# A four-layer graph network in one launch: stages cut into small steps, one fixed turn for all five engines, and a sigmoid formed from exp

## The chip, the cores and the metric

The kernel runs on one core of a Trainium2 chip. A core has a matrix engine (TensorE, in the profile PE, with its weight loads as PEld), a vector engine (VectorE, DVE), an engine for activation functions (ScalarE, ACT), a general engine (GpSimd, POOL) and one that starts transfers (SyncE, SP). Each works through its own row of instructions in order and waits on semaphores for the others. The metric is the device time of one launch in microseconds. Before the change it was 2602.46 us, the median of three runs (2601.76 to 2607.09).

## The reference

The input x is 128 graphs of 128 nodes with 256 features, in single precision. One 128x128 adjacency `adj` serves all. Each of the four layers adds its result to x; each starts with a normalization over the features and a relu:

```python
h = jnp.maximum(_layernorm(x, axis=-1), 0.0)
# layer 0: messages along adj and its transpose, three sigmoid gates per node
msg_in   = (origin*adj @ h + edge_bias)         * sigmoid(h @ gate_weight + bias_gate)
msg_out  = (origin.T*adj @ h + out_edge_bias)   * sigmoid(h @ out_gate_weight + out_bias_gate)
msg_loop = h * sigmoid(h @ loop_gate)
x = x + relu(msg_in + msg_out + msg_loop)
# layer 1: causal attention over the nodes with adj as additive mask, then Wo
# layer 2: three products, each followed by adj*S (S = 1), relu after the first two
#          widths 256 -> 512 -> 1024 -> 256
# layer 3: adj normalized by degree, then Linear(256 -> 512), batch norm over all
#          graphs and nodes, relu, Linear(512 -> 256), batch norm, no relu
```

(The code is shortened; names are those of the reference.) Both batch norms need sums over all graphs, so there is a first pass up to the input of the first batch norm, then a second pass over all graphs, and a last one that writes the output.

## The kernel before

Four graphs make a group; there are 32 groups, and the first pass works on several at once: while layer 2 of group g runs, layer 1 of group g+1, layer 0 of group g+2 and layer 3 of group g-1 fill in between. Each layer is a Python generator, and a `yield` ends a stage. A string gives the order in which stages are emitted (capitals for stages of the current streams, `b` and `d` for those that start the next ones):

```python
TURN = "CCBBCBACDBCABBCABDBACBDDACDCADDCDCBDCADBCBACABCbCBbCBBCBBCBBCBCbBCd"
FIRST = "CCCB" + TURN[2:].replace("C", "", 1)
...
for g in range(NG):
    if g + AHEAD < NG:
        load_x(g + AHEAD)
    ...
    stream = {
        "A": part(layer0, g + 2), "B": bs, "C": layer2(g), "D": ds,
        "b": part(layer1, g + 2), "d": layer3(g),
    }
    for k in FIRST if g == 0 else TURN if g < LAST else FINAL:
        next(stream[k], None)
```

The emitted order is only a wish: a scheduler that comes after it may move an instruction ahead of others of its engine. A few instructions are kept in emitted order by `keep_in_program_order` (the relus of `norm`, the transposes of `cut`), the stores of z are put behind certain loads by `follow`, and `in_turn`, which chains every new instruction to the one before it on its engine, is used for TensorE in the opening stage alone.

All wide products use Strassen's scheme in Winograd's form: seven products in place of eight, in three accumulators (px, py, pz; 2 KB per partition each, one of eight PSUM banks):

```python
def seven(product, put, shape, name, pool=None):
    def kept(pb, i):                       # copy an accumulator away, ScalarE
        t = (pool or w).tile(shape, FP, tag="kept", name=f"{name}_t{i}", bufs=6)
        nc.scalar.copy(t, pb)
        return t
    px = bank(shape, f"{name}_x");  product(0, px, True);  t1 = kept(px, 1);       yield
    py = bank(shape, f"{name}_y");  product(1, py, True);  put((0, 0), py, t1);    yield
    pz = bank(shape, f"{name}_z");  product(4, pz, True);  t5 = kept(pz, 5);       yield
    product(5, px, False);  t2 = kept(px, 2);                                      yield
    product(2, pz, False);  put((0, 1), pz, t2);                                   yield
    product(6, px, False);  put((1, 1), px, t5);                                   yield
    product(3, px, False);  put((1, 0), px, None);                                 yield
```

(Here put several to a line.) A product that goes on in px or pz must wait until the copy or addition of the one before has read it. `put` adds on VectorE and, in layer 2, applies relu on ScalarE. `sums` makes the four sums of quarter matrices that the scheme needs, on VectorE.

`norm` makes the statistics on VectorE, the inverse square root in four small steps on GpSimd, and h by four relus on ScalarE. Three matrices must be turned (h before layer 1, the gated adjacency m of layer 0, the softmax p of layer 1); `swap` sends them out to memory and back with their 32x32 blocks exchanged, and `cut` turns the blocks on VectorE:

```python
# layer 0, groups 2 and on
nc.vector.scalar_tensor_tensor(gs, h[:, b, :], 1.0, gw[:, i, :], ALU.mult, ALU.mult,
                               accum_out=gl[:, k, i : i + 1])       # 12 per group
nc.vector.tensor_tensor(gl, gl, gate_bias, ALU.add)
gt = small.tile([P, n, 3], FP, tag="gt", name=f"gt_{tail}")
nc.scalar.activation(gt, gl, AF.Sigmoid)
yield
... # m = gt0*ain + gt1*aout + gt2*ident (ScalarE, then VectorE); bias = gt0*eb + gt1*oeb
swap(flatT, f"cc_{g}")
yield; ...; yield
cut(cmb.rearrange("p b n -> p (b n)"), flatT, G)
yield
for q in range(bs[0] // 2, (bs[-1] + 1) // 2):
    pm = bank([P, 2, D], f"pm_{g}_{q}")
    for r in range(2):
        b = 2 * q + r
        nc.tensor.matmul(pm[:, r, :], cmbT[:, b, :], h[:, b, :], start=True, stop=True)
    half = slice(2 * q, 2 * q + 2)
    nc.vector.tensor_tensor(bias[:, half, :], pm, bias[:, half, :], ALU.add)
```

The softmax of layer 1 uses `AF.Exp` on ScalarE, four times a group. Names in the profile: p_x, p_y, p_z are accumulators of layer 2 (reading uT, us for the second product, h2T, h2s for the third), pu those of its first, pqv of layer 1's query and value product, pz of layer 3; ps and py are attention's scores and output, pm is layer 0's message (line 616) or the mixing by adj before layer 2 (line 449), pmu the mixing after its first product, pg that of layer 3, pr the last step of layer 2.

Of the kernel before, what the change touches and what calls it, by code (L numbers as in the profile page):

```python
# [22 lines left out]
def kernel(  # L23
# [61 lines left out]
    behind = {}  # L85

# [104 lines left out]
    nc.scalar.activation(table, nhalf[:, 0:1], AF.Sigmoid)  # L191
# [168 lines left out]
    def norm(g, layer, bs=ALL):  # L360
# [4 lines left out]
        for k, b in enumerate(bs):  # L365
            nc.vector.bn_stats(st[:, k, :], xt[:, b, :])  # L366
        for k in range(n):
            nc.vector.bn_aggr(mv[:, k, :], st[:, k, :])  # L368
# [10 lines left out]
        def relus(blocks=False, pinned=False):  # L379

            h = tile_of(g, bs, [P, G, D], "h", f"h{layer}_{g}", 3)
            for k, b in enumerate(bs):
# [6 lines left out]
                relu = nc.scalar.activation(  # L389
                    dst, src, AF.Relu, bias=sh[:, k : k + 1], scale=rs[:, k : k + 1]  # L390
                )
                if pinned:
                    tc.keep_in_program_order(relu)
# [19 lines left out]
    fetched = []  # L413

    def follow(i, name):

        tc.add_manual_dep(
            i, name,
            mybir.DependencyInfo(mybir.DependencyClass.NoSync, mybir.DependencyReason.DATA),
            reason="follow",  # L420
        )

    def swap(blocks, name):

        e = blocks.shape[1] // NQ
        home = scratch.tile([NQ, Q, NQ, e], FP, name=name)
        for i in range(NQ):
            nc.sync.dma_start(
                home[:, :, i, :].rearrange("j r e -> r j e"),
                blocks[i * Q : (i + 1) * Q].rearrange("p (j e) -> p j e", j=NQ),  # L430
            )
        nc.sync.dma_start(blocks, home.rearrange("j r i e -> (j r) (i e)"))
        fetched.append(nc.cur_bb.bb.instructions[-1].name)

    def cut(dst, blocks, nb):

        tc.keep_in_program_order(
            nc.vector.transpose(
                dst.rearrange("p (b i c) -> p b i c", b=nb, i=NQ),
                blocks.rearrange("p (i b c) -> p b i c", i=NQ, b=nb),  # L440
            )
        )

    def mixed(dst, src, aT, name, evicts, bs=ALL):

        for c in range(src.shape[-1] // P):
            pm = bank([P, len(bs), P], f"{name}_{c}")
            for k, b in enumerate(bs):
                nc.tensor.matmul(  # L449
                    pm[:, k, :], src[:, b, c * P : (c + 1) * P], aT, start=True, stop=True  # L450
                )
            evicts[c % len(evicts)](columns(dst, c, bs), pm.rearrange("p b n -> p (b n)"))  # L452

    def sums(engine, a, extra, s3=None):
# [5 lines left out]
        engine.tensor_tensor(s1, a21, a22, ALU.add)  # L460
        engine.tensor_tensor(s2, s1, a11, ALU.subtract)
        engine.tensor_tensor(s4, a12, s2, ALU.subtract)
        engine.tensor_tensor(s3, a11, a21, ALU.subtract)
# [38 lines left out]
    def seven(product, put, shape, name, pool=None):  # L502
# [10 lines left out]
        product(0, px, True)  # L513
        t1 = kept(px, 1)
# [3 lines left out]
        put((0, 0), py, t1)  # L518
        yield
        pz = bank(shape, f"{name}_z")  # L520
        product(4, pz, True)
        t5 = kept(pz, 5)
        yield
        product(5, px, False)
        t2 = kept(px, 2)
        yield
        product(2, pz, False)
        put((0, 1), pz, t2)
        yield
        product(6, px, False)  # L530
        put((1, 1), px, t5)
        yield
        product(3, px, False)
        put((1, 0), px, None)
        yield

    def layer0(g, bs=ALL):

        xt, n, tail = X[g], len(bs), f"{g}_{bs[0]}"
        relus = norm(g, 0, bs)  # L540
        if g >= 2:
            yield
        h = relus(pinned=g >= 1)
# [16 lines left out]
        else:  # L560
            gs = w.tile([P, D], FP, tag="gs", name=f"gs_{tail}", bufs=1)
            for k, b in enumerate(bs):
# [5 lines left out]
                if k == n // 2 - 1:  # L568
                    yield
            nc.vector.tensor_tensor(gl, gl, gate_bias, ALU.add)  # L570
        gt = small.tile([P, n, 3], FP, tag="gt", name=f"gt_{tail}")
        nc.scalar.activation(gt, gl, AF.Sigmoid)
# [9 lines left out]
        for k, b in enumerate(bs):  # L582
            nc.scalar.activation(cmb[:, b, :], ain, AF.Copy, scale=gt[:, k, 0:1])
            nc.vector.scalar_tensor_tensor(
# [6 lines left out]
            nc.vector.scalar_tensor_tensor(dst, one, gt[:, k, 2:3], now, ALU.mult, ALU.add)  # L591
        if g >= 2:
            swap(flatT, f"cc_{g}")
        for k, b in enumerate(bs):
            nc.scalar.activation(bias[:, b, :], eb, AF.Copy, scale=gt[:, k, 0:1])
        yield
        for k, b in enumerate(bs):
            nc.vector.scalar_tensor_tensor(
                bias[:, b, :], oeb, gt[:, k, 1:2], bias[:, b, :], ALU.mult, ALU.add
            )  # L600
        mine = slice(bs[0], bs[-1] + 1)
# [10 lines left out]
        for q in range(bs[0] // 2, (bs[-1] + 1) // 2):  # L612
            pm = bank([P, 2, D], f"pm_{g}_{q}")
            for r in range(2):
                b = 2 * q + r
                nc.tensor.matmul(pm[:, r, :], cmbT[:, b, :], h[:, b, :], start=True, stop=True)  # L616
            half = slice(2 * q, 2 * q + 2)
            nc.vector.tensor_tensor(bias[:, half, :], pm, bias[:, half, :], ALU.add)
        yield
# [5 lines left out]
    def layer1(g, bs=ALL):  # L625
# [5 lines left out]
        relus = norm(g, 1, bs)  # L631
        if n == G:
            yield
        h = relus(swapped, n == G)
# [9 lines left out]
        if n == G:  # L644
            yield
            ex = w.tile([P, 4, 1, T // 2], FP, tag="ex", name=f"hs_{g}", bufs=2)
            hs = sums(nc.vector, quarters_t(hT), ex, ex[:, 3])
# [16 lines left out]
        def put(ij, pb, other):  # L664
# [3 lines left out]
            else:  # L668
                nc.vector.tensor_tensor(dst, pb, other, ALU.add)

# [29 lines left out]
        for k, b in enumerate(bs):  # L700
            for c in range(DC):
# [4 lines left out]
                )  # L706
        p = tile_of(g, bs, [P, G, P], "p", f"p_{g}", 1)[:, bs[0] : bs[-1] + 1, :]
        nc.vector.scalar_tensor_tensor(
            p, ps, 1.0 / D**0.5, maskb[:, None, :].to_broadcast([P, n, P]), ALU.mult, ALU.add
        )  # L710
        nmax = small.tile([P, n], FP, tag="nmax", name=f"nmax_{tail}")
        nc.vector.tensor_reduce(nmax, p, AX.X, ALU.max, negate=True)
        psumr = small.tile([P, n], FP, tag="psumr", name=f"psumr_{tail}")
# [10 lines left out]
        if n == G:  # L724
            swap(flat_p, f"pc_{g}")
        rsum = small.tile([P, n], FP, tag="rsum", name=f"rsum_{tail}")
# [11 lines left out]
        for q in halves:  # L738
            py = bank([P, 2, D], f"py_{g}_{q}")
            for r in range(2):  # L740
                b = 2 * q + r
                nc.tensor.matmul(py[:, r, :], pT[:, b - bs[0], :], v_of(b), start=True, stop=True)
            for r in range(2):
# [4 lines left out]
                )  # L748
        yield
        relus = norm(g, 2, bs)  # L750
        if n == G:
            yield
        h = relus(pinned=n == G)
        yield
        mT = tile_of(g, bs, [P, DC, T], "dT", f"mT_{g}", 2)
        mixed(mT, h, a2T, f"pm2_{tail}", (nc.vector.tensor_copy, nc.scalar.copy), bs)
        if n == G:
            ex = w.tile([P, 3, 1, T // 2], FP, tag="ex", name=f"ms_{g}", bufs=2)
            ms = sums(nc.vector, quarters_t(mT), ex)
# [3 lines left out]
        def put(ij, pb, other):  # L763
# [4 lines left out]
            else:  # L768
                nc.vector.tensor_tensor(dst, pb, other, ALU.add)  # L769
                nc.scalar.activation(dst, dst, AF.Relu)  # L770
# [17 lines left out]
        mixed(uT, u, a2T, f"pmu_{tail}", (nc.vector.tensor_copy,), bs)  # L788
        if bs[-1] == G - 1:
            ex = w.tile([P, 3, HC1 // 2, T // 2], FP, tag="us", name=f"us_{g}", bufs=1)  # L790
            US[g] = sums(nc.vector, quarters_t(uT), ex)
        yield

    def layer2(g):
# [8 lines left out]
        def wide(q):  # L803
            def put(ij, pb, other):
# [3 lines left out]
                if other is None:  # L808
                    nc.scalar.activation(dst, pb, AF.Relu)
                    mine = slice(2 * q, 2 * q + 2)  # L810
                    sums(
# [3 lines left out]
                else:  # L815
                    nc.vector.tensor_tensor(dst, pb, other, ALU.add)  # L816
                    nc.scalar.activation(dst, dst, AF.Relu)  # L817
# [7 lines left out]
        def put_s(ij, pb, other):  # L825
# [6 lines left out]
            else:  # L832
                nc.vector.tensor_tensor(dst, pb, other, ALU.add)

        yield from wide(0)
        late = wide(1)
        for _ in range(6 if g == LAST else 7):
            yield next(late)
        third = seven(rows_by_half(h2s, SETS["3"], P), put_s, [P, 2, P], f"p3_{g}")
        yield next(third)  # L840
        yield from late if g == LAST else ()
        yield from third
        for q in range(G // 2):
            pr = bank([P, 2, D], f"pr_{g}_{q}")
            nc.tensor.matmul(pr, a2T, S[0][:, 2 * q : 2 * q + 2, :], start=True, stop=True)  # L845
            nc.vector.tensor_tensor(
                xt[:, 2 * q : 2 * q + 2, :], pr, xt[:, 2 * q : 2 * q + 2, :], ALU.add
            )
        nc.gpsimd.dma_start(X3[g].rearrange("(b n) d -> n b d", n=P), xt)
        yield  # L850

    def layer3(g):
# [3 lines left out]
        for bs in parts:  # L856
            relus = norm(g, 3, bs)
            if g < LAST:
                yield
            h = relus(pinned=g < LAST)  # L860
            yield
        gT = tile_of(g, parts[0], [P, DC, T], "dT", f"gT_{g}", 2)
        for i, bs in enumerate(parts):
            mixed(gT, h, ahT, f"pg_{g}_{i}", (nc.vector.tensor_copy,), bs)
            if g < LAST:
                ex = w.tile([P, 3, 1, T // 2], FP, tag="ex", name=f"gs_{g}", bufs=2)
                gs = sums(nc.vector, quarters_t(gT), ex)
# [4 lines left out]
        def put(ij, pb, other):  # L872
# [13 lines left out]
            if done.count(j) == 2:  # L886
                if g < LAST - 1:
                    for jj in range(2):
                        nc.vector.bn_stats(stats1[:, 2 * j + jj, g, :], z[j][:, jj, :])

        if g < LAST:
            yield from seven(columns_by_half(gs, SETS["b"], 0), put, [P, 2, T // 2], f"pz_{g}")
            at = len(nc.cur_bb.bb.instructions)
            for j in (1, 0):
                nc.sync.dma_start(Z[g][:, 2 * j : 2 * j + 2, :], z[j])
            for i in nc.cur_bb.bb.instructions[at:]:
                for name in fetched[-2:]:
                    follow(i, name)
            yield
            return  # L900
        for i, j in (0, 0), (1, 0), (0, 1), (1, 1):
# [9 lines left out]
            put((i, j), pb, None)  # L911
# [12 lines left out]
    TURN = "CCBBCBACDBCABBCABDBACBDDACDCADDCDCBDCADBCBACABCbCBbCBBCBBCBBCBCbBCd"  # L924
    FIRST = "CCCB" + TURN[2:].replace("C", "", 1)


    FINAL = "CCCCCCCCDCCCCCCCCCCDCCCCDDdDDddDdDdDDdddd"
    US = {}
    AHEAD = 3  # L930

# [12 lines left out]
    for k in FILL:  # L944
# [3 lines left out]
        else:  # L948
            next(stream[k])
# [3 lines left out]
    for _ in range(2):  # L953
        next(bs)
    for g in range(NG):
# [8 lines left out]
        for k in FIRST if g == 0 else TURN if g < LAST else FINAL:  # L964
# [246 lines left out]
```

## Time and profile before

| | |
|---|---|
| median of 3 runs | 2602.46 us |
| span of the profiled execution | 2598.9 us, 40812 instructions |
| first pass, groups 1 to 30 | from about 140 to about 2273 us |
| second and last pass | from about 2330 us to the end |
| HBM traffic | 105 MB read, 99 MB written, 78 GB/s on average |
| loads of ScalarE's function tables | 61 in the loop, 78.3 us of ScalarE |

The profile comes from one execution. Its page gives the busy time of each engine, the span in 40 slices, the chain of work that ended last followed backward, and groups of instructions by line of the kernel. A line such as `L816 DVE TENSOR_TENSOR h2T<-p_z,p_t 128x512 f32<-128x512 f32 x64 | 43.6, 682 | 122.5 <-ACT h L389 108.3` reads: source line 816, on VectorE, writes h2T from p_z and p_t, 64 times; busy 43.6 us in all, 682 ns each; VectorE was idle 122.5 us just before these, 108.3 of it until ScalarE ended h at line 389. A timeline lists instructions by time: start, duration of the run of equal ones, and in brackets the idle time before it with its releaser. In a list of waits stand the total in us, the number of times and the longest. A single-precision matmul of the program stands as two records in the trace.

### The profile page before, as it was taken

To read this page: it belongs to the slowest core of one execution; us is meant where nothing else is said; L and a number is where in the kernel's file an instruction comes from. 1 tells how busy PE (TensorE), PEld (TensorE's weight loads), DVE (VectorE), ACT (ScalarE), POOL (GpSimd) and SP (SyncE) were. 2 spreads that over 40 slices of the span, in tenths; PEclk is the share of its full clock that TensorE was granted. 3 is DMA by queue.
4 is the path that set the end of the run, shared out by engine and by line. 5 is a ranking of instruction groups with operands and counts; after the bars stand their busy time and mean duration, and the time that the engine had idled before them with its cause. 6 is when DMAs were issued, how large, how long until landed. Compare 5 with 4: busy or idle time off the path is not lost.

```text
span 2598.9 us, 40812 instructions
## 1 busy us (share of the span) xinstructions
PE 2520.7 (97%) x14832; PEld 2236.0 (86%) x14832; DVE 1921.9 (74%) x4795; ACT 1259.5 (48%) x2547; POOL 271.5 (10%) x563
## 2 busy tenths in 40 slices
PE   7999999999999999999999999999999999999996
PEld 6788888888888888888888888888888888888875
DVE  7677777777777777777777777877777777558886
ACT  4444444444445444444444454444444444337766
POOL 2110011111001110111111011100111110000001
PEclk9999999999999999999999999999999999999998
DMA  3112211222222112112222222122112221125559
GB/s 133 45 52 66 65 46 54 65 66 58 62 61 66 57 58 66 54 50 61 66 63 60 58 66 58 56 65 59 51 54 66 66 57 49 33 99 217 178 186 388
DMA packets 115180, 206.54 MB, mean 79 GB/s; under 512 B 11538, under 2 KB 77092, under 8 KB 111012
## 3 DMA queue, kind: packets, MB, share of 16 engines
q1 hardware_dynamic: 108404, 180.80, 22.3%
q0 software_dynamic: 6432, 23.07, 2.5%
q8 instruction: 117, 1.92, 0.3%
q14 instruction: 83, 0.68, 0.1%
q10 hardware_dynamic: 144, 0.07, 0.0%
HBM read 105.20 MB, written 98.70 MB: 78 GB/s over the span
## 4 chain that ended last, share of the span: by engine, by line
PE 91%; DVE 4%; ACT 2%; DMA 1%; issue 1%; POOL 0%; SPq 0%; ACTq 0%; DVEq 0%; POOLq 0%
PE p_x L494 16%; PE p_x L477 9%; PE p_z L494 8%; PE pz_x L494 4%; PE p_z L477 4%; PE pmu L449 4%; PE p_y L494 4%; PE po_x L1084 4%; PE pu_x L477 4%; PE pz_z L494 2%; PE pm L616 2%; PE pm L449 2%; PE pqv_x L654 2%; PE pg L449 2%; PE p_y L477 2%; PE pr L845 2%
## 5 line engine op out<-in xcount | busy, mean ns | idle before, releaser
L389 ACT ACTIVATE h<-x,sh,rs 128x256 f32<-128x256 f32 x512 | 265.6, 589 | 69.9 <-POOL sh L375 57.8
L494 PE MATMUL p_x<-uT,w 128*128 128x256 f32 x1024 | 247.0, 379 | 0.0
L509 ACT COPY p_t<-p_x 128x512 f32<-128x512 f32 (+1 forms) x192 | 97.4, 507 | 299.4 <-PE p_x L494 291.2
L494 PEld LDWEIGHTS p_x<-uT,w 128*128 128x128 f32 x1024 | 192.0, 190 | 38.0 <-issue 14.8
L817 ACT ACTIVATE h2T<-h2T 128x512 f32<-128x512 f32 x192 | 120.9, 630 | 198.1 <-DVE h2T L816 198.1
L366 DVE BATCH_NORM_STATS2 st<-x 128x6 f32<-128x256 f32 x512 | 182.2, 411 | 0.2
L564 DVE SCALAR_TENSOR_TENSOR gs<-h,gw 128x256 f32<-128x256 f32 x360 | 151.1, 420 | 41.0 <-ACT h L389 35.6
L372 POOL TENSOR_SCALAR rs<-mv 128x4 f32<-128x4 f32 x124 | 29.7, 240 | 1287.6 <-DVE mv L368 1237.0
L816 DVE TENSOR_TENSOR h2T<-p_z,p_t 128x512 f32<-128x512 f32 x64 | 43.6, 682 | 122.5 <-ACT h L389 108.3
L373 POOL TENSOR_TENSOR rs<-rs,nhalf 128x4 f32<-128x4 f32 x124 | 128.7, 1038 | 0.0
L477 PEld LDWEIGHTS p_x<-w,h2T 128*128 128x128 f32 x1024 | 124.5, 192 | 3.3
L494 PE MATMUL p_z<-us,w 128*128 128x256 f32 x512 | 125.8, 379 | 0.0
L477 PE MATMUL p_x<-w,h2T 128*128 128x128 f32 x1024 | 124.8, 275 | 0.0
L494 PE MATMUL p_x<-us,w_s 128*128 128x256 f32 x512 | 121.3, 379 | 3.0 <-ACT p_t L509 3.0
L494 PE MATMUL p_x<-uT,w_s 128*128 128x256 f32 x512 | 121.5, 380 | 2.0 <-DVE h2T L816 2.0
L494 PE MATMUL p_z<-us,w_s 128*128 128x256 f32 x512 | 121.0, 379 | 0.0
L494 PE MATMUL p_y<-uT,w 128*128 128x256 f32 x512 | 120.9, 379 | 0.0
L449 PE MATMUL pmu<-a2T,u 128*128 128x128 f32 x1024 | 119.6, 275 | 0.0
L452 DVE COPY uT<-pmu 128x512 f32<-128x512 f32 (+1 forms) x132 | 88.4, 674 | 40.7 <-PE pmu L449 40.7
L449 PEld LDWEIGHTS pmu<-a2T,u 128*128 128x128 f32 x1024 | 116.9, 192 | 0.0
L770 ACT ACTIVATE u<-u 128x512 f32<-128x512 f32 x93 | 58.6, 630 | 116.7 <-DVE u L769 116.7
L494 PEld LDWEIGHTS p_y<-uT,w 128*128 128x128 f32 x512 | 97.3, 190 | 13.2
(331 smaller groups left out, 6061.1 us busy)
## 6 DMA issues: line engine op xcount, KB each, us to landing
z<-zo SPq DMA_DIRECT2D x62, 512.0 KB, 4.1
zi<-z SPq DMA_DIRECT2D x31, 1024.0 KB, 4.9
x<-x POOLq DMA_DIRECT2D x32, 512.0 KB, 3.5
x<-in_x_dram SPq DMA_DIRECT2D x31, 512.0 KB, 3.9
hc<-h SPq DMA_DIRECT2D x120, 128.0 KB, 2.5
h<-hc SPq DMA_DIRECT2D x30, 512.0 KB, 3.5
out_dram<-x3i SPq DMA_DIRECT2D x30, 512.0 KB, 10.5
x3i<-x SPq DMA_DIRECT2D x20, 512.0 KB, 6.5
```

The source lines that it names most:

```text
L366: nc.vector.bn_stats(st[:, k, :], xt[:, b, :])
L373: nc.gpsimd.tensor_tensor(rs, rs, nhalf[:, :n], ALU.pow)
L389: relu = nc.scalar.activation(dst, src, AF.Relu, bias=sh[:, k : k + 1], scale=rs[:, k : k + 1])
L449: nc.tensor.matmul(pm[:, k, :], src[:, b, c * P : (c + 1) * P], aT, start=True, stop=True)
L452: evicts[c % len(evicts)](columns(dst, c, bs), pm.rearrange("p b n -> p (b n)"))
L477: nc.tensor.matmul(pb[:, rr, :], a_r[r][:, c, rr * P : (rr + 1) * P], b_r[r][:, c, :wide], start=(first and rr == 0 and c == 0), stop=(c = ...
L494: nc.tensor.matmul(pb[:, jj, :], b_r[r][:, c, at : at + P], a_r[r][:, c, :], start=(first and jj == 0 and c == 0), stop=(c == nk - 1), ski ...
L509: nc.scalar.copy(t, pb)
L564: nc.vector.scalar_tensor_tensor(gs, h[:, b, :], 1.0, gw[:, i, :], ALU.mult, ALU.mult, accum_out=gl[:, k, i : i + 1],)
L770: nc.scalar.activation(dst, dst, AF.Relu)
L817: nc.scalar.activation(dst, dst, AF.Relu)
L1084: nc.tensor.matmul(pb, BW2R[r][:, c, :], a_r[r][:, c, :], start=(first and c == 0), stop=(c == FC // 2 - 1), skip_group_check=True,)
```

## The change

It has two parts. The first cuts the stages into small steps and fixes the order. New `yield SPLIT` lines stand within the stages, between one engine's operation and the next engine's. `stage` and `step` run a generator to the end of its stage where the old manner is wanted (the opening, group 31, the second pass). In groups 0 to 30 each letter of a new turn of 196 letters is one small step; in groups 1 to 30 `in_turn` then chains the new instructions on all five engines, so that the scheduler no longer chooses. The marks that kept single instructions in order are dropped, and `follow` with them. The second part replaces the sigmoid of the gates by 1/(1+exp(-z)): exp on ScalarE, an addition and a reciprocal on VectorE. It is meant to spare the reloads of ScalarE's tables between sigmoid and the exp of softmax.

```diff
+    SPLIT = "within a stage"
...
-    nc.scalar.activation(table, nhalf[:, 0:1], AF.Sigmoid)
+    nc.scalar.activation(table, nhalf[:, 0:1], AF.Exp)
...
         for k, b in enumerate(bs):
             nc.vector.bn_stats(st[:, k, :], xt[:, b, :])
+            if k % 2:
+                yield SPLIT
...
-                if pinned:
-                    tc.keep_in_program_order(relu)
+                if k == 1 and n == G:
+                    yield SPLIT
...
         engine.tensor_tensor(s1, a21, a22, ALU.add)
+        yield SPLIT
         engine.tensor_tensor(s2, s1, a11, ALU.subtract)
+        yield SPLIT
...
         px = bank(shape, f"{name}_x")
         product(0, px, True)
+        yield SPLIT
         t1 = kept(px, 1)
         yield
         py = bank(shape, f"{name}_y")
         product(1, py, True)
-        put((0, 0), py, t1)
+        yield SPLIT
+        yield from put((0, 0), py, t1)
...
-        nc.scalar.activation(gt, gl, AF.Sigmoid)
+        nc.scalar.activation(gt, gl, AF.Exp, scale=-1.0)
+        yield SPLIT
+        nc.vector.tensor_scalar(gt, gt, 1.0, None, ALU.add)
+        nc.vector.reciprocal(gt, gt)
...
         third = seven(rows_by_half(h2s, SETS["3"], P), put_s, [P, 2, P], f"p3_{g}")
-        yield next(third)
-        yield from late if g == LAST else ()
+        if g == LAST:
+            for part in (late,) * 6 + (third,):
+                yield from stage(part)
+        yield from late
         yield from third
...
-            at = len(nc.cur_bb.bb.instructions)
             for j in (1, 0):
                 nc.sync.dma_start(Z[g][:, 2 * j : 2 * j + 2, :], z[j])
-            for i in nc.cur_bb.bb.instructions[at:]:
-                for name in fetched[-2:]:
-                    follow(i, name)
...
-    TURN = "CCBBCBACDBCABBCABDBACBDDACDCADDCDCBDCADBCBACABCbCBbCBBCBBCBBCBCbBCd"
-    FIRST = "CCCB" + TURN[2:].replace("C", "", 1)
+    TURN = (
+        "DCDCCCCCBDBBBBBBBBABBBDDDAABBBBCCDDAAAABBDCCCBBCCBBACCAADDDDAADDAAACCDBA"
+        "CCCCCCCCCCCCDDDABCCCCCCBBBADDBBBCCBBBBCCDCCACCCCCCAAAAABBbbbBBBBBDDBBBCC"
+        "CCCbCCbBBBBBBBBBDDBBBBBBCDBDDBCCCdBBBBCCCdBBdBBBBBbB"
+    )
+    BEGUN = 6
+    PINNED = tuple(
+        getattr(mybir.EngineType, e) for e in ("PE", "DVE", "Activation", "Pool", "SP")
+    )
...
-    for _ in range(2):
+    for _ in range(BEGUN):
         next(bs)
...
-        for k in FIRST if g == 0 else TURN if g < LAST else FINAL:
+        for k in TURN if g < LAST else ():
+            at = len(nc.cur_bb.bb.instructions)
             next(stream[k], None)
+            if g:
+                in_turn(at, PINNED)
+        for k in FINAL if g == LAST else ():
+            step(stream[k])
```

The number of matmuls, their shapes and the data moved stay as they were.

## The prediction

> **What bounds the kernel now.** I read the page first (part 1, shares; part 2, slices), then the chain that ended last, then one repeating stretch of the timeline, then the waits of the weight loads. The page and the chain:
>
> ```profile
> PE 2520.7 (97%) x14832; PEld 2236.0 (86%) x14832; DVE 1921.9 (74%) x4795; ACT 1259.5 (48%) x2547; POOL 271.5 (10%) x563
> ...
> PEclk9999999999999999999999999999999999999998
> ...
> PE 91%; DVE 4%; ACT 2%; DMA 1%; issue 1%; POOL 0%; SPq 0%; ACTq 0%; DVEq 0%; POOLq 0%
> ```
>
> TensorE is the bound, at full granted clock, and there is little left to take: the chain is TensorE for 91%. How little is read from one group. In the timeline of TensorE alone the last addition of layer 2 (pr) starts at 992.32, 1063.52 and 1134.72 us: groups 1 to 29 each take 71.20 us, to 0.01 us. Within such a group:
>
> ```profile
> 1034.63 0.59 PE L494 MATMUL p_x<-uT,w 128*128 128x256 f32 x2
> 1036.09 1.97 PE L616 MATMUL pm<-h,m 128*128 128x256 f32 x8 [0.86 <-DVE m L438]
> ...
> 1058.16 1.95 PE L477 MATMUL p_x<-w_s,h2T 128*128 128x128 f32 x16
> 1059.95 3.74 PE L449 MATMUL pmu<-a2T,u 128*128 128x128 f32 x32
> 1063.52 1.88 PE L845 MATMUL pr<-s,a2T 128*128 128x512 f32 x4
> 1065.24 1.89 PE L494 MATMUL p_x<-uT,w 128*128 128x256 f32 x8
> 1066.97 1.89 PE L494 MATMUL p_y<-uT,w 128*128 128x256 f32 x8
> ```
>
> The differences of the starts are the true pace (durations overlap): 1.73/8 = 0.216 us for a 128x256 record, 1.79/16 = 0.1117 for 128x128, 1.72/4 = 0.43 for 128x512. A group holds 198, 220 and 4 of them (wide products 112, query and value 14, layer 2's first 28, layer 3's 28, py and pm 16; third products 112, value halves 28, pm2, pg, ps 48, pmu 32; pr 4). 198 x 0.216 + 220 x 0.1117 + 4 x 0.43 = 42.8 + 24.6 + 1.7 = 69.1 us. So 71.20 - 69.1 = 2.1 us a group is not work, and that is all that reordering can give there. Where it sits, in totals over the run:
>
> ```profile
> PEld pm L616 <- PE p_x L494: 35.8, 29, 1.3
> PEld p_x L494 <- issue: 14.8, 62, 0.2
> PEld pr L845 <- issue: 14.8, 62, 0.2
> PEld pto L1166 <- ACT o L1158: 14.2, 29, 4.0
> PEld pz_z L494 <- ACT pz_t L509: 12.2, 29, 0.4
> PEld pz_x L494 <- DVE zo L876: 9.3, 29, 0.3
> PEld py L742 <- issue: 9.3, 29, 0.3
> PEld pz_x L494 <- ACT pz_t L509: 7.8, 29, 0.3
> PEld pqv_x L654 <- ACT pqv_t L509: 6.4, 30, 0.2
> ```
>
> Over half is one wait: pm, 1.23 us in each group. The timeline of all engines says why:
>
> ```profile
> 1033.18 0.67 DVE L816 TENSOR_TENSOR h2T<-p_z,p_t 128x512 f32<-128x512 f32 x1
> 1033.97 1.35 DVE L745 SCALAR_TENSOR_TENSOR x<-py,rsum,x 128x256 f32<-128x256 f32 x3
> 1035.23 0.70 DVE L438 STREAM_TRANSPOSE m<-m 128x512 f32<-128x512 f32 x1
> ```
>
> VectorE makes m (the last transpose) only after three additions that themselves wait for py, and TensorE has two matmuls left to put in between. The pz and pqv lines are products that take up an accumulator right after it was to be copied out: 0.2 to 0.4 us each. The two issue lines around pr are loads hidden behind the long pr matmuls and cost nothing; pto belongs to the last pass.
>
> **What the Trainium skill says.** "Perfetto Trace Analysis", section "Identifying the Most-Contended Engine", warns that matmul occupancy overstates how full TensorE is; here it is right in kind (durations of 0.379 us start every 0.216), which is why I count starts. The same page, section "Tensor Engine Instruction", says that VectorE, ScalarE and GpSimd are strictly first in, first out; the DVE lines above agree (m stands behind x). "ScalarE: Activation LUTs", section "Table sets: the hidden batching unit", puts exp and sigmoid into different sets and relu and copy into each; the trace agrees, with 31 loads at the Exp line and 30 at the Sigmoid line. Its section "What ACT_TABLE_LOAD costs" gives about 1283 ns and a drain of 1380 more; the load is 1283 ns here, but the next activation starts 0.01 us after it and no drain is seen.
>
> **The change, part by part.** (1) Sigmoid from exp. It takes away 30 + 31 loads, 38.5 + 39.8 = 78.3 us of ScalarE, 2.6 us a group, and adds an addition of one and a reciprocal on 128x12 to VectorE (a 128x4 reciprocal is 0.178 and a 128x12 addition 0.164 us, so some 0.35 us a group). ScalarE is busy 33.5 of a group's 71.2 us and no TensorE wait above names the table: on the end directly 0. It makes room on ScalarE just where softmax's exponentials and pz's copies stand.
>
> (2) The fixed turn. The program of the new kernel shows one order for groups 1 to 30 on every engine. I lay TensorE's new order end to end at the paces above (0 = first wide product, 69.1 = the next group's) and check each hand-over by hand with start-to-start times from the trace: VectorE 0.60 for 512 elements, 0.33 for 256 statistics, 0.34 + 0.1 for a gate sum, 1.16 for the large transpose; ScalarE 0.49 for a relu of 256, 0.47 to 0.54 for 512; GpSimd's four steps after a normalization 2.2 to 2.6; TensorE to VectorE 0.27, to ScalarE 0.20, back about 0.1.
> - pm: the transpose of m now stands after layer 2's sums, done at about 45.5; pm is due at 46.2. The 1.23 us goes.
> - pz and pqv: between a product and the next use of its accumulator now stand one or two whole products. pz_z is due at 32.2 with its copy at 27.1; pqv_z at 10.5, copy at 9.4; the third pqv_x at 14.0, VectorE's addition at 13.6. These go, some 0.7 us.
> - py at 36.5: exponentials end at 21.5, the trip through memory takes 6.9 us (1023.4 to about 1030.2 in the old trace), the transpose is in VectorE's row at 30.9. No wait.
> - The closest ones: pg at 5.2 to 6.1 uses relus that end at 3.8 to 5.3; p_y at 1.73 needs uT at 1.4; ps needs at 17.46 a copy of qv that ScalarE can make only after four relus of the next group, done at 17.54. I count 0.1 us for ps and 0.1 for what a hand check misses.
> So a group takes 69.1 + 0.2 = 69.3, to be on the safe side: 29 x (71.20 - 69.3) = 55.1 us. Group 30 took 68.75 us from pr to pr and lacks layer 0's pm (8 x 0.216 = 1.7): 69.3 - 1.7 = 67.6, another 1.2.
>
> (3) Group 0 is not pinned. Transposes of h now precede the first product; h is ready at 67.1 and the product started at 67.64, so nothing is lost. Its waits (3.0, 2.3, 0.8 and 0.4 us) hang on the first loads and may move either way: 0, give or take 3. Group 31, the last pass and the start keep their orders: 0.
>
> Sum: 2602.46 - 55.1 - 1.2 = 2546.2; the hand check itself gave 0.1 less of wait a group, 3 us. I take 2545.
>
> **Rivals.**
> - A. A rigid order breaks at one link. VectorE has 51.8 us of work in 69.1, but waits in line: if one operation stands ahead of its input, all behind it wait, and the wait comes back each group. Candidates: the copy of qv before ps, the relus before pg. For: their margins are 0.0 to 0.5 us. Against: a chain that is late by d costs d once a group. At 0.5 us a group the time is 2557, at 1.5 it is 2587; at 2.1 nothing is gained.
> - B. VectorE or ScalarE becomes the bound. Against: 75% and about 50% of a group, and the change takes work from ScalarE. It would take over 17 us more on VectorE to reach this. About 1% likely.
> - C. Nothing but the floor: all waits go, and group 0's too. 2602.5 - 30 x 2.1 - 3 = 2536. That is the least that this change can reach, since all matmuls stay.
> - D. The clock sinks with a fuller TensorE. The granted clock is 0.995 at 97% already; for it speaks nothing in the trace.
>
> **Range and chances.** The 2% line is at 2550.4, a saving of 52 us, or 1.73 us a group of the 2.1. The estimate lies 5 us beyond it, which is 0.18 us a group: the size of one link that I judged too kindly. Hence 0.65 for faster by over 2%, 0.30 for within, and 0.05 for slower (a link that costs over 3.8 us a group, which no margin above suggests). The range has the floor at its lower end and a link of 0.9 us at the upper one: 2537 to 2570.
>
> **What would show it.** In the changed kernel: pr starts repeat every 69.1 to 69.4 us; the pm line is gone from the waits of the weight loads; the pz and pqv lines are gone or under 0.1 us; a single table load is left and ScalarE's busy time is down by about 78 us; VectorE's is up by 5 to 12; the granted clock stays. Group 0 ends within 3 us of 139.7. The prediction is wrong if a new wait of 0.5 us or more appears 30 times, at ps, pg or p_y first, or if the group keeps 71 us without any wait in view, which would mean that the paces above are not the floor.

## The result, and the profile after

The changed kernel takes 2535.36 us, the median of four runs (2534.36 to 2536.71), against 2603.86 us for the kernel before in the runs beside it (2601.76 to 2607.09): a ratio of 0.9736, with a 95% interval of 0.9719 to 0.9753. It is faster by 2.6%. The prediction said 2545 and a range from 2537 to 2570, so the direction was right and the gain was bigger than I allowed for.

The page of the changed kernel, parts 1, 2 and 4 (engines, granted clock of TensorE in 40 slices, shares of the chain that ended last; line numbers are each version's own, so the same line of code has another number here than before):

```profile
span 2534.7 us, 40786 instructions
...
PE 2483.4 (98%) x14832; PEld 2246.1 (89%) x14832; DVE 1970.5 (78%) x4861; ACT 1180.4 (47%) x2486; POOL 311.4 (12%) x563
...
PEclk9999999999999999999999999999999999999998
...
PE 94%; DMA 2%; DVE 2%; ACT 1%; POOL 0%; issue 0%; SPq 0%; DVEq 0%; POOLq 0%; ACTq 0%
```

The same 14832 matmul records, the same clock, 64.2 us less span. ScalarE is busy 79.1 us less (the loads of its tables), VectorE 48.6 us more. The chain is TensorE for 94% instead of 91%. Its timeline around the end of a group and around pm:

```profile
1031.62 1.02 PE L873 MATMUL pr<-s,a2T 128*128 128x512 f32 x2
1032.48 1.95 PE L440 MATMUL pmu<-a2T,u 128*128 128x128 f32 x16
1034.27 1.02 PE L873 MATMUL pr<-s,a2T 128*128 128x512 f32 x2
1035.13 1.95 PE L440 MATMUL pmu<-a2T,u 128*128 128x128 f32 x16
1036.91 0.60 PE L490 MATMUL p_x<-uT,w 128*128 128x256 f32 x2
...
1081.29 1.95 PE L473 MATMUL p_z<-w_s,h2s 128*128 128x128 f32 x16
1083.07 1.89 PE L630 MATMUL pm<-h,m 128*128 128x256 f32 x8
...
1099.78 1.03 PE L473 MATMUL pu_x<-w_s,mT 128*128 128x256 f32 x4
1100.64 0.59 PE L873 MATMUL pr<-s,a2T 128*128 128x512 f32 x1
```

From pr to pr it is 1100.64 - 1031.62 = 69.02 us, and all groups from 1 to 29 repeat that to 0.01. None of these rows has a bracket (idle time); pm follows the product ahead of it at that product's own pace (1.78 us for 16 records). What the weight loads still wait for:

```profile
PEld pmu L440 <- issue: 21.8, 91, 0.2
PEld pto L1217 <- ACT o L1209: 13.8, 28, 4.0
PEld pmu L440 <- PE pmu L440: 7.4, 31, 0.2
PEld pqv L696 <- ACT hT L412: 5.2, 2, 4.7
PEld pgw L268 <- issue: 4.5, 1, 4.5
```

The columns are total us, times, longest. The lines of pm at layer 0, of pz and of pqv_x that came in every group are gone. The two pmu lines stand beside the long matmuls of pr and cost nothing, since the group has no time over. The rest is the last pass (pto) and the opening (pqv, pgw, once or twice each).

Where the 64.2 us between the two profiled spans come from: 29 x (71.20 - 69.02) = 63.2, and group 30 went from 68.75 to 67.63, 1.1 more. That leaves nothing for the opening, group 0, group 31 and the last pass; the first product of group 1 starts at 139.66 us before and 139.67 after (that these two are so close is luck of the two executions, as the opening below shows).

### The profile page after: what moved, and what is told of

It is laid out like the page before. It is cut to its first block, busy times and chain, and to the rows that moved or that the text cites. A ratio compares the mean times of both kernels' runs of the same rounds, so it can differ in the third digit from the quotient of the medians.

```text
span 2534.7 us, 40786 instructions
## 1 busy us (share of the span) xinstructions
PE 2483.4 (98%) x14832; PEld 2246.1 (89%) x14832; DVE 1970.5 (78%) x4861; ACT 1180.4 (47%) x2486; POOL 311.4 (12%) x563
## 4 chain that ended last, share of the span: by engine, by line
PE 94%; DMA 2%; DVE 2%; ACT 1%; POOL 0%; issue 0%; SPq 0%; DVEq 0%; POOLq 0%; ACTq 0%
PE p_x L490 17%; PE p_x L473 9%; PE p_z L490 9%; PE pmu L440 5%; PE p_z L473 4%; PE p_y L490 4%; PE po_x L1134 4%; PE pz_x L490 4%; PE pu_x L473 4%; PE p_y L473 2%; PE pg L440 2%; PE py L764 2%; PE ps L720 2%; PE pm L630 2%; PE pm L440 2%; PE pr L873 2%
## 5 line engine op out<-in xcount | busy, mean ns | idle before, releaser
L375 POOL TENSOR_SCALAR rs<-mv 128x4 f32<-128x4 f32 x124 | 37.2, 300 | 1378.8 <-DVE mv L371 1365.4
L440 PEld LDWEIGHTS pmu<-a2T,u 128*128 128x128 f32 x1024 | 124.2, 192 | 29.6 <-issue 21.8
L490 PEld LDWEIGHTS p_x<-uT,w_s 128*128 128x128 f32 x512 | 97.1, 190 | 13.4 <-DVE h2T L842 0.3
L490 PEld LDWEIGHTS p_z<-us,w_s 128*128 128x128 f32 x512 | 97.3, 190 | 13.2
```

Of the source, the lines that this page charges most:

```text
L440: nc.tensor.matmul(pm[:, k, :], src[:, b, c * P : (c + 1) * P], aT, start=True, stop=True)
L490: nc.tensor.matmul(pb[:, jj, :], b_r[r][:, c, at : at + P], a_r[r][:, c, :], start=(first and jj == 0 and c == 0), stop=(c == nk - 1), ski ...
```

## The experiments

"Repeat" is the time from the first pr of one group to that of the next in groups 1 to 29, read from the timeline of TensorE.

| run | gate | turn | kept in groups 1 to 30 | repeat, us | median, us | ratio to before (95%) |
|---|---|---|---|---|---|---|
| before | Sigmoid | old | single marks | 71.20 | 2603.2 to 2603.9 | 1 |
| e2 | exp | old | single marks | 70.73 | 2588.83 | 0.9943 (0.9928 to 0.9958) |
| f4 | Sigmoid | old | all five engines | 78.6 to 80.3 | 2838.15 | 1.0899 (1.0883 to 1.0915) |
| e3 | exp | new | nothing | 69.93 | 2562.56 | 0.9844 (0.9829 to 0.9858) |
| f3 | exp | new | TensorE, ScalarE | 69.94 | 2561.50 | 0.9838 (0.9824 to 0.9853) |
| f2 | exp | new | TensorE, VectorE | 69.11 | 2539.05 | 0.9750 (0.9736 to 0.9765) |
| f6 | exp | new | the gate sums alone | 69.02 | 2535.44 | 0.9740 (0.9726 to 0.9753) |
| e1 | Sigmoid | new | all five engines | 69.15 | 2536.95 | 0.9745 (0.9731 to 0.9760) |
| after, again (g1) | exp | new | all five engines | 69.02 | 2536.56 | 0.9744 (0.9730 to 0.9757) |

Below: what each was to tell, then the four that probe the room in the order and the opening.

**The sigmoid put back (e1).** The edit in the changed kernel:

```diff
-    nc.scalar.activation(table, nhalf[:, 0:1], AF.Exp)
+    nc.scalar.activation(table, nhalf[:, 0:1], AF.Sigmoid)
...
-        nc.scalar.activation(gt, gl, AF.Exp, scale=-1.0)
+        nc.scalar.activation(gt, gl, AF.Sigmoid)
         yield SPLIT
-        nc.vector.tensor_scalar(gt, gt, 1.0, None, ALU.add)
-        nc.vector.reciprocal(gt, gt)
```

> The changed kernel with its turn and its kept order, but the gate formed again by the Sigmoid function, so that two table loads a group (about 1.28 us each) come back to ScalarE and the add of 1 and the reciprocal leave VectorE. Theory (the order makes the gain, the exp none of it in groups 1 to 30): the loads fall ahead of the exp of the softmax and ahead of the gate, where the products have about 1 us of room; repeats stay at 69.0 to 69.1 us, time 2535, between 2531 and 2540. Rival (the exp freed the room that the order uses): every group loses 1.3 to 2.6 us, time 2573 to 2611.

Repeats of 69.15 us: the loads cost 0.13 us a group, not 1.3 to 2.6. The timeline of ScalarE in that run (a load, then the four exponentials; a load, then the gate):

```profile
1053.14 1.28 ACT L740 ACT_TABLE_LOAD   x1
1054.44 0.40 ACT L740 ACTIVATE pT<-p,nmax 128x128 f32<-128x128 f32 x1
...
1056.62 1.28 ACT L574 ACT_TABLE_LOAD   x1
1057.92 0.21 ACT L574 ACTIVATE gt<-gl 128x12 f32<-128x12 f32 x1
```

Both loads are there in full, and ScalarE takes them up beside the products. Its one trace on TensorE is a line in the waits, p_z for the copy p_t on ScalarE, 7.5 us in all, 29 times. 29 x 0.13 = 3.8 us was lost, and the median is only 1.6 above that of the changed kernel (which itself came out at 2535.36 and, in g1, at 2536.56). The opening came out shorter with it: the first product of group 0 starts at 71.06 us instead of 76.46. That set off the last runs below.

**The exp alone (e2).** The mirror image: the kernel before, with exp, an addition and a reciprocal in place of Sigmoid, and the table loaded once.

> The kernel before, with the gate formed from exp as the only edit; the scheduler orders as freely as before. Theory (table loads lay beside the products): ScalarE's busy time falls by about 78 us, the time stays at 2602, between 2595 and 2608. Rival (the loads were what made the products wait): TensorE's waits on the groups fall and the time drops by 20 us or more, to 2582 or less.

Neither. The time fell by 14.5 us, while I had said it would stay. Its first line in the waits of the weight loads, which had 35.8 us before:

```profile
PEld pm L618 <- PE p_x L494: 23.1, 29, 0.8
```

A line of TensorE ahead of py in the kernel before:

```profile
1102.62 1.46 PE L494 MATMUL p_x<-uT,w 128*128 128x256 f32 x6
```

And the timeline of TensorE around pm in e2:

```profile
1097.91 1.03 PE L494 MATMUL p_x<-uT,w 128*128 128x256 f32 x4
1099.04 1.97 PE L744 MATMUL py<-qv,p 128*128 128x256 f32 x8
1100.84 1.03 PE L494 MATMUL p_x<-uT,w 128*128 128x256 f32 x4
1102.29 1.97 PE L618 MATMUL pm<-h,m 128*128 128x256 f32 x8 [0.42 <-DVE m L438]
```

In the kernel before, six of these p_x records ran ahead of py and two behind it; here it is four and four. From py's start to the transpose of m on VectorE it is the same 2.4 us in both (1104.03 to 1106.43 before, 1099.04 to 1101.45 here). TensorE merely has two more records of 0.216 us to do in that time, 0.43 of the 0.47 us by which the repeat fell. So, as these rows read, it isn't the lighter ScalarE that gave most of the 14.5 us: a scheduler that was told of other instructions laid the row of TensorE otherwise, to our luck. (The two rows of TensorE differ in some other places, too, and no run has the old row with exp in it, so this is read and not tested.)

**The turn without the keeping (e3).** The edit takes away `if g: in_turn(at, PINNED)`. The row of TensorE stays the same, instruction for instruction; those of VectorE and ScalarE differ.

> The changed kernel with its new turn of 196 steps, but groups 1 to 30 are not kept in the order in which they are given: the scheduler places VectorE's and ScalarE's work by its own lights, while the row of TensorE comes out the same instruction for instruction. Theory (the wait of before came from what stood in VectorE's row, not from the turn): most of the gain is lost, repeats of 70.3 to 71.5 us, time 2572 to 2610, with a wait of the weight loads on VectorE's transposes back in the list. Rival (the finer steps alone bring the order): repeats of 69.0 to 69.3, time 2535 to 2545.

Between the two: 69.93, so the new turn and exp alone bring 1.27 of the 2.18 us a group and the keeping 0.91. The wait that is left is not pm's, as I had thought, but a new one. The first of its waits:

```profile
PEld pqv_x L671 <- DVE qv L686: 30.3, 29, 1.1
```

And the timeline of ScalarE, VectorE and TensorE in one group of it:

```profile
1061.94 2.07 ACT L392 ACTIVATE h<-x,sh,rs 128x256 f32<-128x256 f32 x4 [1.20 <-POOL sh L378]
...
1062.57 0.43 DVE L567 SCALAR_TENSOR_TENSOR gs<-h,gw 128x256 f32<-128x256 f32 x1 [1.37 <-ACT h L392]
...
1062.92 0.69 DVE L686 TENSOR_TENSOR qv<-pqv_z,pqv_t 128x512 f32<-128x512 f32 x1
1063.52 0.41 DVE L453 TENSOR_TENSOR gs<-gT 128x256 f32<-128x256 f32 x1
1063.86 0.68 DVE L686 TENSOR_TENSOR qv<-pqv_x,pqv_t 128x512 f32<-128x512 f32 x1
...
1064.59 0.70 PE L671 MATMUL pqv_x<-hT,m_qk_s 128*128 128x256 f32 x2 [0.64 <-DVE qv L686]
```

Read it from below. TensorE wants the accumulator pqv_x, which VectorE's addition at 1063.86 still has to read. That addition stands third behind a gate sum (gs from h), which stood idle 1.37 us until ScalarE had made its h. The addition's own product was complete at 1062.2 and its copied summand before that. One operation that came too early in a row held up all behind it.

**Which row needs it (f2, f3).** The list of kept engines cut down, once to TensorE and VectorE, once to TensorE and ScalarE:

```diff
-        getattr(mybir.EngineType, e) for e in ("PE", "DVE", "Activation", "Pool", "SP")
+        getattr(mybir.EngineType, e) for e in ("PE", "DVE")            # f2
+        getattr(mybir.EngineType, e) for e in ("PE", "Activation")     # f3
```

> The changed kernel with only TensorE and VectorE kept in the given order in groups 1 to 30; ScalarE, GpSimd and the queue of SyncE are left to the scheduler. The run without any keeping lost 0.91 us a group, in a wait of qv's first accumulator on VectorE's qv addition. Theory (VectorE's row is what the keeping mends): repeats of 69.0 to 69.1 us, time 2535, between 2532 and 2539. Rival (ScalarE's row needs it as much): a new wait on ScalarE of 0.3 us or more a group, time 2543 or more.

> The mirror of the run before: only TensorE and ScalarE kept, VectorE left to the scheduler. Theory (VectorE's row is what the keeping mends): the wait of qv's first accumulator on VectorE's qv addition stays at about 1.0 us a group, repeats of 69.9 us, time 2562, between 2557 and 2567. Rival (ScalarE's row led VectorE's astray): repeats of 69.4 or less, time 2547 or less.

VectorE it is. With its row kept, the repeat is 69.11 and no wait of 0.3 us a group is on the list; with ScalarE's kept instead, all is as without any keeping (69.94, the pqv_x line at 30.5 us). f2 ends a hair beyond the upper ends that I had set (69.1 and 2539). The 0.09 us a group between f2 and the changed kernel is what the other three rows add. It stands at ps: from its start to the next product it is 1.87 us in f2 (1051.12 to 1052.99) and 1.79 in the changed kernel (1053.48 to 1055.27). The second half of ps needs the copy of qv, and in f2 the scheduler put another copy ahead of it:

```profile
1050.90 0.57 ACT L505 COPY p_t<-p_x 128x512 f32<-128x512 f32 x1
1051.37 0.58 ACT L684 COPY qv<-pqv_x 128x512 f32<-128x512 f32 x1
```

In the changed kernel the copy of qv comes first (1053.58, p_t at 1054.04).

**One kind of operation kept (f6).** The sharpest form of that reading: nothing kept but the gate sums, twelve in each group, in e3.

```diff
-    nc.vector.scalar_tensor_tensor(gs, h[:, b, :], 1.0, gw[:, i, :], ...)
+    tc.keep_in_program_order(
+        nc.vector.scalar_tensor_tensor(gs, h[:, b, :], 1.0, gw[:, i, :], ...))
```

> The run with the new turn left free, and one thing kept: the gate sums of layer 0 (gs from h and gw) stand in VectorE's row behind what was given ahead of them. In the free run one of them stood ahead of qv's additions and waited 1.37 us for ScalarE's relus; qv's first accumulator waited 1.04 us a group for the addition behind it. Theory (one operation at the head of VectorE's row is the whole of what the keeping mends in the new turn): that wait goes, repeats of 69.0 to 69.3 us, time 2537, between 2533 and 2545. Rival (it moves to the next operation in a row that the scheduler still orders): repeats of 69.5 or more, time 2550 or more.

Repeats of 69.02 and 2535.44 us: as fast as the changed kernel. The timeline of VectorE in that run:

```profile
1047.64 0.68 DVE L686 TENSOR_TENSOR qv<-pqv_z,pqv_t 128x512 f32<-128x512 f32 x1
1048.24 0.41 DVE L455 TENSOR_TENSOR gs<-gs,gT 128x256 f32<-128x256 f32 x1
1048.57 0.68 DVE L686 TENSOR_TENSOR qv<-pqv_x,pqv_t 128x512 f32<-128x512 f32 x1
1049.17 0.41 DVE L567 SCALAR_TENSOR_TENSOR gs<-h,gw 128x256 f32<-128x256 f32 x1
```

The gate sum now stands behind both additions, pqv_x is free at 1049.2, and TensorE takes it at 1049.85 without a wait. (gs<-gT, too, has the name gs: it is a sum for layer 3, another buffer.) The Trainium skill, "Perfetto Trace Analysis", section "Tensor Engine Instruction", calls VectorE, ScalarE and GpSimd strictly first in, first out. e3 and f6 agree: the 0.91 us a group hung on where the gate sums stand. That it was the first of them alone, one operation of 0.43 us, is read from e3, whose list has no other new wait that comes in every group. f6 doesn't show it by itself: it keeps all twelve, and TensorE's row is the same, but VectorE's and ScalarE's change further down as well.

**The old turn kept (f4).** Is keeping an order enough, whatever the order? The kernel before, with `in_turn` on all five engines around its 67 coarse stages (`PINNED` names them, as in the change):

```diff
+            at = len(nc.cur_bb.bb.instructions)
             next(stream[k], None)
+            if 0 < g < LAST:
+                in_turn(at, PINNED)
```

> The kernel before, Sigmoid and old turn of 67 coarse steps, with the one edit that all five engines are kept in the order in which it is given in groups 1 to 30. Theory (without the fine steps a stage's whole chain stands in one piece in each row, and a copy that TensorE needs soon stands behind work that isn't due): worse than free, each group longer than 71.2 us by 1 to 6 us, time 2630 to 2780. Rival (keeping any sensible order is enough): repeats of 69.0 to 70.0, time 2535 to 2565.

It is slower by 9%, worse than my worst figure: repeats of 78.6 to 80.3 us. Its four dearest waits:

```profile
PEld pz_z L494 <- ACT pz_t L509: 81.9, 29, 3.0
PEld pz_x L494 <- ACT pz_t L509: 71.7, 29, 2.5
PEld pqv_x L654 <- DVE qv L669: 54.1, 29, 1.9
PEld pqv_x L654 <- ACT pqv_t L509: 25.4, 30, 0.9
```

And one of those of pz_x in the timeline of ScalarE and TensorE:

```profile
1124.03 0.40 ACT L721 ACTIVATE pT<-p,nmax 128x128 f32<-128x128 f32 x1 [2.84 <-DVE nmax L712]
...
1125.59 0.56 ACT L509 COPY pz_t<-pz_x 128x512 f32<-128x512 f32 x1
...
1126.20 1.22 PE L494 MATMUL pz_x<-gs,bw1T_s 128*128 128x256 f32 x2 [2.07 <-ACT pz_t L509]
```

A whole stage stands in one piece in each row: the four exponentials, 1.56 us, and their wait for VectorE's maximum stand ahead of the copy pz_t, for which TensorE waits. The fine steps are what lets such a copy be put ahead; the keeping without them did harm here.

The waits are not the whole loss. The mean granted clock of this run is 0.963 against 0.995 before, and the timeline of TensorE goes on:

```profile
1129.93 2.07 PE L494 MATMUL pz_z<-gs,bw1T 128*128 128x256 f32 x4 [1.65 <-ACT pz_t L509]
1131.79 2.48 PE L494 MATMUL p_z<-us,w_s 128*128 128x256 f32 x8
```

Four records of pz_z take 1.86 us to the next start, 0.465 each instead of 0.216. The view by windows has the clock (stretch; its length; busy time of PE, PEld, DVE, ACT and POOL; granted clock; share of the DMA engines; GB/s):

```profile
1126.20:1133.03 6.83, 5.18 (x11) 3.70 (x12) 6.04 (x15) 4.78 (x12) 0.00 (x0) 0.50 0.49 115
```

TensorE was granted half its clock for these 6.83 us. Such a stretch of 6.83 or 3.41 us comes once in each of the groups 1 to 29 of this run, beside these waits, and in no other run between groups 1 and 30. The repeats come back every five groups (80.25, 79.39, 78.95, 78.73 and 78.62 us), the stretch is 3.41 us long in the last of the five, and by how much it reaches past the start of pz_z changes with them. In that part TensorE does half the work, so half of it is an estimate of what the clock costs: 3.1 us in the longest group and 1.4 in the shortest, out of the 7.4 to 9.1 us that a group takes longer than before. The rest are the waits. Whether the waits bring on the low clock is not shown: the two come together in each group, and no run separates them.

**How much room the kept order has (e4).** The last relu of layer 0's norm is given three times in the changed kernel; the output is the same, the two extra relus are pure delay, right ahead of the copy of qv:

```diff
-                nc.scalar.activation(dst, src, AF.Relu, ...)
+                for _ in range(3 if layer == 0 and g >= 3 and k == 3 else 1):
+                    nc.scalar.activation(dst, src, AF.Relu, ...)
```

> The changed kernel as it is, with the last relu of layer 0's norm given three times instead of once in groups 3 to 31 (same values written again): 0.98 us more on ScalarE, right ahead of the copy of qv that the products of ps wait for. Theory (the kept order has next to no room at its closest link: the copy ends 0.2 us before ps needs it): each group loses 0.98 less 0.2, about 0.75 us, repeats of 69.8, time 2557, between 2551 and 2564. Rival (ScalarE is idle over half of the time and takes it up): time 2535, between 2532 and 2540.

2570.37 us, above the 2564 that I had allowed; ratio 0.9873 (0.9860 to 0.9886), repeats of 70.21: 1.19 us lost in each group. The first of its waits is new:

```profile
PEld ps L721 <- ACT qv L685: 32.4, 29, 1.1
```

ScalarE's relus in the changed kernel:

```profile
1051.60 2.08 ACT L392 ACTIVATE h<-x,sh,rs 128x256 f32<-128x256 f32 x4 [3.77 <-POOL sh L378]
```

The timeline of ScalarE and TensorE at that place in e4:

```profile
1063.67 3.34 ACT L393 ACTIVATE h<-x,sh,rs 128x256 f32<-128x256 f32 x6 [3.77 <-POOL sh L378]
1066.92 0.56 ACT L685 COPY qv<-pqv_x 128x512 f32<-128x512 f32 x1
...
1067.54 1.16 PE L721 MATMUL ps<-hT,qv 128*128 128x128 f32 x8 [0.93 <-ACT qv L685]
```

Six relus take 3.34 us where four take 2.08, so the delay was 1.26 and not 0.98, and TensorE lost 1.19 of it. The room at this link is 0.07 us. The rival (an engine that is idle over half of the time takes it up) falls: ScalarE stands idle 3.77 us right ahead of these relus and can't use it, for it waits for the norm.

**The opening (e5, f1, g1, g2).** The first product of group 0 starts at 67.64 us before and at 76.46 after, and group 0 makes that up. Is it lost? (This start differs between executions. Seven profiles, of the changed kernel, g1, e3, e4, f2, f3 and f6, have the same instructions in the same order on TensorE, VectorE, ScalarE and GpSimd up to it and start it between 72.89 and 77.53 us; the two with the opening of before, before and f4, at 67.64 and 70.27.) In e5 ScalarE, too, is kept in the given order in the opening:

```diff
-    KEPT = (mybir.EngineType.PE,)
+    KEPT = (mybir.EngineType.PE, mybir.EngineType.Activation)
```

> The changed kernel, with ScalarE kept in the given order in the opening too (there TensorE alone was kept), so that the copy of hT for group 0 no longer stands behind the relus of group 1. Theory (the opening's 8.8 us later first product of group 0 comes in part from that place in ScalarE's row, and is hidden only because group 0 then waits less): the first product of group 1 comes 2 to 8 us earlier than at 139.7 us, time 2531, between 2527 and 2533. Rival (group 0's end is set by something else, such as the loads of X or VectorE): the first product of group 0 moves, the first product of group 1 doesn't, time 2534 to 2537.

2536.32 us, ratio 0.9744 (0.9728 to 0.9760): nothing gained. The first product of group 0 came at 76.29. The wait for hT that it was to take away (4.43 us) fell to 0.5 at most, but another stood up in its place, as the waits of that run show:

```profile
PEld pl L558 <- ACT h0T L412: 5.9, 2, 5.2
```

Neither theory had that. In f1 the opening of before is given back in two places: Sigmoid in groups 0 and 1 (and its table loaded at the start), and the mark on group 1's relus.

```diff
+        if g < 2:
+            nc.scalar.activation(gt, gl, AF.Sigmoid)        # else exp, + 1, reciprocal
...
+                if layer == 0 and g == 1:
+                    tc.keep_in_program_order(relu)
```

> The changed kernel in groups 1 to 30, with the opening of the kernel before given back in two places: the gate of groups 0 and 1 formed by Sigmoid, and the relus of group 1's first norm kept behind what was given ahead of them. The run with the table back had its first product of group 0 at 71.06 us instead of 76.46, and its group 0 took as long. Theory (the 8.8 us are lost in the opening alone and carry through to the end): first product of group 0 at 66 to 69 us, repeats of 69.02, time 2527, between 2525 and 2531. Rival (the opening's time is taken back in group 0, as between before and after): time 2533 or more.

2531.72 us (0.9723, 0.9707 to 0.9739), just above what I expected. Then once more, beside the changed kernel:

> The changed kernel once more, without an edit, on the same chip as the run below: 2535, between 2532 and 2538.

> The changed kernel with the opening of the kernel before (Sigmoid in groups 0 and 1, group 1's relus kept), once more, beside the changed kernel on one chip. Theory (the opening's 7.2 us earlier first product reaches the end): 4 to 8 us below the changed kernel. Rival (the first look was the luck of the first loads): within 2 us of it.

2530.45 us (0.9718, 0.9705 to 0.9732) against 2536.56 for the changed kernel on the same chip: 6.1 us better than it, and the fastest version here. The first product of group 0 starts at 69.20 in g2 and 75.39 in g1, 6.2 us apart; from there to the first pr it is 57.92 us in g2 and 57.91 in g1. So what the opening gains reaches the end. Which of the two edits gives how much of it, no run tells.

## Why the prediction was right and wrong

- **What bounds it** (TensorE at full clock, 2.1 us a group of no work): right. With no wait left, the group takes 69.02 us. My floor of 69.1 was the sum 42.77 + 24.57 + 1.72 = 69.06 rounded up, and the paces in it were rounded too: with 1.73/8 and 1.79/16 as they stand it is 69.15. Starts with two decimals give the floor to about 0.1 us.
- **The failed step is the size put on part 2: "69.1 + 0.2 = 69.3, to be on the safe side".** By hand I had found one wait, 0.08 us at ps, counted 0.1 for it and another 0.1 "for what a hand check misses". Neither is there: measured 0.0. It was close at ps, though: e4 puts its room at 0.07 us, where I had it late by 0.08, and in f2 0.09 us are lost there. The term cost 29 x 0.2 = 5.8 us of the estimate and the rounded floor 29 x 0.08 = 2.3, together 8.1: the sum of 2546.2 becomes 2538.1. The last 2.7 us are less than the runs of before differ among themselves.
- **The range's lower end** failed with it. I called 2536 "the least that this change can reach" and set the end at 2537, so a kernel with all waits gone was bound to fall at or beyond the edge of the range, and my own hand check was only 0.08 us a group away from that. The allowance belonged into the upper side of the range, not into its middle.
- **Part 1, "on the end directly 0"**: right for the table loads in the new order, to 0.13 us a group (e1). But e2 shows that the edit alone would have moved the old kernel by 14.5 us, by way of the scheduler. "Directly" hid that.
- **Part 2, the list of waits**: pm, pz and pqv all went, as told link by link. What the keeping itself does was not in my list: without it, it is qv's addition behind a gate sum that costs 0.91 us (e3, f6).
- **Part 3, group 0, "0, give or take 3"**: the end of group 0 moved by 0.01 us, but by two errors that cancel, and so exactly only by luck, as that start alone spreads over 4.6 us between executions. "The product started at 67.64, so nothing is lost" is wrong: it started 8.8 us later in the profiled executions. Part of that is from exp in the opening (e1, with Sigmoid, has 71.06, below all seven), and part, as I read it but did not test alone, from group 1's relus ahead of the copy of hT. And group 0 got 8.8 us shorter: its idle time on TensorE fell from 6.5 to 1.4 us, and the rest I have not split up.
- **Rival A**: its rule, that a chain late by d costs d once a group, held on e4 (1.26 in, 1.19 out), and f4 is what it looks like when the order is bad. In the changed kernel no link is late. B and D didn't come: VectorE is busy 78% of the span, and the clock stays at 9 in every slice but the last (where it did sink, in f4, TensorE was less full, at 91%). VectorE's busy time rose by 48.6 us instead of the 5 to 12 that I named; in f6 the same 4861 instructions show 1936.5 us, so most of the rise is how closely they follow one another, not work, and it cost nothing. **C came true.**

Open: what brings on the half clock in f4, and how the later start of the opening divides between exp and group 1's relus.

## What to carry to other kernels

In a kernel whose bound engine is 97% busy, find the period of the loop and the sum of its work; if a walk through the new order finds no wait, or next to none, predict the sum itself and keep doubts for the range. When a row of an in-order engine makes the bound one wait, look one place ahead of the operation that it waits for: keeping one kind of operation from standing too early was worth as much here as keeping five engines, and fixing an order that is too coarse cost 9%, a fifth to a third of it at half clock by estimate. An edit that only adds or removes small operations can move the time through the scheduler, so compare the rows of the bound engine before giving a gain to the engine that was relieved.

## What the runs showed of the hardware that I had not expected

- Relus that write the same buffer again start 0.63 us apart ((3.34 - 2.08) / 2), those that write different ones 0.49. A delay that is put in by repeating an operation is larger than that operation's pace.
- At the switch of ScalarE's table the trace of e1 shows the load's 1.28 us and nothing after it: the first exponential starts at 1054.44, 0.02 us after the load at 1053.14 ends. The Trainium skill, "ScalarE: Activation LUTs", section "What ACT_TABLE_LOAD costs", has a drain beside the load; no run here shows it.
- In f4 the granted clock fell to half for 6.83 or 3.41 us in each group, with TensorE idle for 1.65 to 2.6 us at a time just before or within the stretch; in e4, where it is idle for 0.93 us at a time, it didn't.
